# Two thirds of the cross-attention values by seven block products, W2 in single units, norm pieces in fewer steps

## The chip, the cores and the metric

The kernel runs on one core of a Trainium2 chip. A core has five engines that run at the same time and wait for each other through semaphores: TensorE (PE in the profile) multiplies matrices and writes to PSUM banks, VectorE (DVE) and ScalarE (ACT) do elementwise work, GpSimd (POOL) does a little of that and issues some transfers, SyncE (SP) issues most transfers. "PEld" are TensorE's weight loads, which run beside its matmuls. The metric is the device time of one execution in microseconds (us): 1362.22 us, the median of three runs from 1362.15 to 1363.08. All arithmetic is in fp32.

## The reference

A decoder layer on x of 16 batches of 112 tokens with 512 features. Three parts are added to x in turn, each applied to the normalized x:

```python
x = x + attn(layernorm(x))                      # 16 heads of 32, low-rank factors
x = x + xattn(layernorm(x), ctx_2048, mask)     # ctx: 16 x 375 x 512
x = x + ffn(layernorm(x))                       # 512 -> 2048 -> 512

# xattn
q, k, v = hs @ Wq.T + bq, at @ Wk.T + bk, at @ Wv.T + bv     # at = ctx
scores = clip(where(attend, clip(q . k / sqrt(32)), -10000), -50, 50)
probs  = softmax(scores);  probs = probs / (probs.sum() + 1e-8)
delta  = rs * ((probs . v) @ Wo.T + bo)
delta  = (delta - mean) / sqrt(var + eps) * ln_gamma + ln_beta
# ffn
out = fwht(silu(x @ W1.T) * (x @ W3.T)) @ W2.T               # fwht over 2048
```

The Hadamard transform (fwht) of the hidden layer is applied to W2 instead, once for all tokens. Each of the 16 batches has 375 context tokens whose keys and values (512 features each) have to be computed: this is the work that the change touches.

## The kernel before

The profiled function is `decoder_layer` with its body `finite_layer`; a second path for input that isn't finite exists and doesn't run. There are three stages: self-attention to about 304 us, cross-attention to about 823 us, the feed-forward part to the end.

TensorE's instructions stand in an order written out by hand (`tc.manual_schedule`). The other engines' order is made by a scheduler, which places each instruction by when it expects its operands; on each engine instructions then start strictly in that order. `tc.issue_after(x)` keeps instructions behind x in it. A class `Filler` holds a queue of generators, each a series of small pieces of TensorE work; `fill(us)` runs pieces of it worth so many microseconds, `drain` all that are left. `mixed(a, b, n)` takes pieces of two generators in turn after n pieces of the first.

**The cross loop.** Iteration b attends batch b and, as filling, makes keys and values of batch b+1. The 375 tokens are three chunks of 125 (KP). A step (b, kc) of `Cross.step` has the scores of chunk kc (matmuls L925), their exp on ScalarE (L1326) with a scale and a bias per token that carry the mask (tiles `scl`, `bia`, laid out by token and chunk), the weighing of the values of the chunk before (L936), and the sum of the exponentials on VectorE (L1356). At kc = 0 the batch before is divided: `key_sums` (L947) sums the exponentials over tokens into one PSUM bank, four reciprocals (L1368) read it, and one operation (L1369) multiplies. Behind each step the filling runs.

**Values and keys.** `token_rows` (L898) makes the values of a chunk: 4 matmuls of 512 columns with the chunk's context as weights, then a copy on VectorE (L903). `Seven.biased` (L1005) makes the keys of a batch (512 features, 376 columns, the last one a zero) by seven products of blocks of 256 features and 188 tokens, in place of eight, as Strassen's method does. For this it needs sums of blocks of the weight (tile `xks`, once) and of the context (tile `kt`, L975, four operations of 2 x 188 columns per batch). A product is 4 matmuls of 188 columns. VectorE gathers the products into `kT` (L1058 to L1092), some with the keys' bias bk or with the difference of its halves, dbk. Two of the three held banks accumulate several products. The context of batch b+2 is loaded by one transfer at the start of iteration b (L1214), and GpSimd clears the last column.

**Other work in the loop.** Queries of two batches at odd b (L880). At b = 0, 4, 8 the output projection of a group of four batches (L909) and afterwards its norm and residual (`finish` pieces: at bl = b mod 4 > 0, two per step). W2 has two phases. Up to b = 8 its four halves (`W2Half`) are loaded, multiplied with a small Hadamard matrix (L1627, scaled by L1628) and combined by butterflies (L1643, L1644), one pair per step. From b = 9 on, `W2Piece` reads four quarters of two units each (2 x 256 columns) from what the halves stored (L1660, tile `w2i`), makes six sums of them (L1671 to L1686, tiles `w2i` and `w2o`) and stores each (L1669), two operations per step: four pieces. At b = 14 and 15 the first blocks of the feed-forward part are loaded, and their sums (L965) made.

**Buffers.** PSUM tag "mm" has 3 banks, which nearly all filling and the key sums take in turn. Weights, `xks`, `kt`, W2's tiles and the first feed-forward blocks share 8 slots of 8 KB a partition (`weight`); context and keys share 4 (`big`); values have 5; rows of 512, among them the mask and the first normalized tiles, take slots of a ring (`row`).

## Time and profile before

| | |
|---|---|
| three runs | 1362.15, 1362.22, 1363.08 us |
| profiled execution | 1362.72 us |
| span of its profile | 1360.9 us |
| granted TensorE clock | 0.998 of full speed |
| busy: PE, DVE, ACT, POOL | 1340.7, 820.6, 440.6, 38.0 us |
| L898 on the context (values, cross) | 178.8 us in 384 records |
| L1005 (keys, cross) | 106.8 us in 600 records |
| context loads | 16 of 750 KB, 4.8 us to landing |
| W2 piece loads, stores | 16 of 256 KB, 24 of 256 KB |

A row of the page's groups reads: line, engine, operation, output <- input by tile names, shapes (for a matmul the weights' rows x columns, then the output), number of records; busy us, mean ns of one; idle time of the engine just before them, and what ended it. Each fp32 matmul leaves two records. Rows of the waits read: who waited, for what, the total in us, how often, the longest. Rows of the timeline read: start in us, length in us, engine, line, operation, and how many records are drawn together. "SPq" is SyncE's queue, which holds the issue of transfers.

### The profile page before, as it was taken

Reading aid. Unit: us, or ns where it says so; the run is one execution under the profiler, and the core shown is the slowest. Engines: PE = TensorE matmul, PEld = TensorE weight load, DVE = VectorE, ACT = ScalarE, POOL = GpSimd, SP = SyncE. Lnnn points to the kernel's source line nnn. Section 1 sums busy time; section 2 is a strip of 40 time slices with the busy share of each in tenths; the row PEclk is TensorE's granted clock in tenths of the full one; section 3 lists DMA queues with packets and bytes.
Section 4 is the critical chain, followed back from the end, with each engine's and each line's share of the span. In section 5 each row is a group of like instructions: output and inputs, shape, how many; then the busy total and the mean of one; then the engine's idle time right before and its main releaser. Section 6 shows DMA issues by size and latency. Waiting matters only on the chain.

```text
span 1360.9 us, 20404 instructions
## 1 busy us (share of the span) xinstructions
PE 1340.7 (99%) x8472; PEld 834.1 (61%) x8472; DVE 820.6 (60%) x1571; ACT 440.6 (32%) x859; POOL 38.0 (3%) x68
## 2 busy tenths in 40 slices
PE   8999999999999999999999999999999999999997
PEld 5587776665767577756777765545555555555553
DVE  4487768735565686669675668557653245554332
ACT  3355453643444334433545452201110011111000
POOL 2000100310000100000000000000000000000000
PEclk9999999999999999999999999999999999999999
DMA  7000022110103011103342111111031122322201
GB/s 249 1 1 1 22 80 71 31 47 24 55 24 124 16 55 62 55 1 109 108 136 97 39 48 32 47 46 47 32 124 62 47 62 70 92 77 79 92 0 57
DMA packets 63898, 82.44 MB, mean 61 GB/s; under 512 B 3105, under 2 KB 48177, under 8 KB 61365
## 3 DMA queue, kind: packets, MB, share of 16 engines
q1 hardware_dynamic: 62128, 77.83, 17.4%
q0 software_dynamic: 672, 1.62, 0.4%
q8 instruction: 69, 1.13, 0.3%
q10 hardware_dynamic: 996, 1.59, 0.3%
q14 instruction: 33, 0.26, 0.1%
HBM read 65.83 MB, written 15.20 MB: 60 GB/s over the span
## 4 chain that ended last, share of the span: by engine, by line
PE 94%; DVE 4%; ACT 1%; DMA 1%; issue 1%; DVEq 0%; ACTq 0%; POOLq 0%
PE mm L898 15%; PE mm L1005 14%; PE gate L1538 12%; PE mm L909 7%; PE ys L1538 7%; PE gate L1472 6%; PE mm L880 6%; PE mm L1538 5%; PE sc L925 5%; PE ys L936 4%; PE ys L1472 4%; PE mm L1472 3%; PE sc L1192 2%; PE mm L841 1%; PE mm L1627 1%; PE mm L947 1%
## 5 line engine op out<-in xcount | busy, mean ns | idle before, releaser
L898 PE MATMUL mm<-xv,cT 128*125 128x512 f32 x384 | 178.8, 602 | 0.8 <-DVE v L903 0.8
L1326 ACT ACTIVATE e<-sc,bia,scl 125x896 f32<-125x896 f32 x64 | 68.4, 1094 | 171.3 <-PE sc L925 171.3
L898 PEld LDWEIGHTS mm<-xv,cT 128*125 128x125 f32 x384 | 68.4, 187 | 76.4 <-issue 71.8
L1330 ACT ACTIVATE sc<-sc,limit,nscl 125x896 f32<-125x896 f32 x96 | 102.6, 1068 | 0.0
L1538 PE MATMUL gate<-t,f 128*128 128x448 f32 x256 | 101.5, 539 | 0.0
L1356 DVE TENSOR_TENSOR es<-es,e 125x896 f32<-125x896 f32 x64 | 68.4, 1090 | 49.1 <-ACT e L1326 49.1
L1472 PE MATMUL gate<-h,f 128*128 128x448 f32 x224 | 86.6, 540 | 0.0
L1538 PE MATMUL gate<-xyT,f 128*128 128x448 f32 x192 | 80.1, 540 | 0.0
L1538 PEld LDWEIGHTS gate<-t,f 128*128 128x128 f32 x256 | 48.8, 190 | 47.4 <-issue 46.9
L1162 ACT ACTIVATE e<-sc,mx 112x112 f32<-112x112 f32 x256 | 64.3, 402 | 41.7 <-DVE mx L1158 41.7
L1538 PE MATMUL ys<-t,f 128*128 128x448 f32 x192 | 77.4, 539 | 0.0
L1005 PEld LDWEIGHTS mm<-kt,xks 128*128 128x128 f32 x360 | 59.1, 190 | 15.3 <-issue 14.8
L1472 PEld LDWEIGHTS gate<-h,f 128*128 128x128 f32 x224 | 42.6, 190 | 41.2 <-issue 40.8
L1554 ACT COPY u<-gate 128x448 f32<-128x448 f32 x16 | 8.5, 531 | 182.3 <-PE gate L1538 109.4
L1005 PE MATMUL mm<-kt,xks 128*128 128x188 f32 x360 | 63.5, 324 | 0.0
L1538 PEld LDWEIGHTS ys<-t,f 128*128 128x128 f32 x192 | 36.6, 190 | 35.6 <-issue 35.4
L1484 DVE TENSOR_TENSOR h<-h,h 128x896 f32<-128x896 f32 x32 | 32.8, 1086 | 40.9 <-PE ys L1472 31.6
L1538 PEld LDWEIGHTS gate<-xyT,f 128*128 128x128 f32 x192 | 36.1, 190 | 34.3 <-issue 33.7
L898 PE MATMUL mm<-wv,xyT 128*112 128x512 f32 x128 | 56.9, 595 | 0.0
L925 PEld LDWEIGHTS sc<-q,kT 32*125 32x125 f32 x1536 | 46.2, 183 | 15.5 <-issue 13.2
L925 PE MATMUL sc<-q,kT 32*125 32x112 f32 x1536 | 54.7, 279 | 0.0
L1538 PE MATMUL mm<-xyT,f 128*128 128x448 f32 x128 | 53.4, 540 | 0.0
(237 smaller groups left out, 2211.2 us busy)
## 6 DMA issues: line engine op xcount, KB each, us to landing
f<-in_f_w SPq DMA_DIRECT2D x64, 256.0 KB, 3.2
f<-blocks SPq DMA_DIRECT2D x14, 1024.0 KB, 4.8
cT<-in_ctx SPq DMA_DIRECT2D x16, 750.0 KB, 4.8
w<-in_f_w SPq DMA_DIRECT2D x4, 1024.0 KB, 6.1
w<-w SPq DMA_DIRECT2D x4, 1024.0 KB, 4.6
w2i<-w SPq DMA_DIRECT2D x16, 256.0 KB, 4.1
blocks<-w2o SPq DMA_DIRECT2D x12, 256.0 KB, 2.4
blocks<-w2i SPq DMA_DIRECT2D x12, 256.0 KB, 2.4
```

Source lines behind the costliest of these rows:

```text
L880: nc.tensor.matmul(acc[:, :n], w[:, c, ts(j, P)], src[:, c, :], start=(c == 0), stop=(c == C - 1))
L898: nc.tensor.matmul(acc[:n, :], src[:, c, :], w[:, c, :], start=(c == 0), stop=(c == C - 1))
L909: nc.tensor.matmul(acc, xyT[:, c, ts(t, P)], w[:, c, :], start=(c == 0), stop=(c == C - 1))
L925: nc.tensor.matmul(views[i // 2][:, i % 2, j, :], k_of(i, j), q_of(i, j), start=True, stop=True)
L936: nc.tensor.matmul(y[ts(i, DH), j, :], v[:, HG * j + i, :], es[i // 2][:n, i % 2, j, :], start=first and j == 0, stop=last, skip_group_che ...
L1005: nc.tensor.matmul(acc[:, m], lhs[:, k, ts(m, P)], rhs[:, k], start=first and m == 0 and k == 0, stop=k == 1, skip_group_check=True,)
L1162: nc.scalar.activation(e[:, i, j, :], sc[:, i, j, :], AF.Exp, scale=SCALE, bias=mx[:, i, j : j + 1],)
L1326: nc.scalar.activation(es[i], sc, AF.Exp, scale=scl[:, n : n + 1], bias=bia[:, n : n + 1])
L1330: nc.scalar.activation(sc, sc, AF.Relu, scale=nscl[:, n : n + 1], bias=limit[:KP, :1], accum_out=low[:KP, 2 * n + i : 2 * n + i + 1],)
L1356: self.last = nc.vector.tensor_tensor(total, total, late[3][i][:KP], ALU.add).ins
L1472: nc.tensor.matmul(banks[m][bank], o[:, c, ts(m, P)], t[:, c, :], start=first and c == 0, stop=c == UNITS - 1, skip_group_check=True,)
L1538: nc.tensor.matmul(bank, o[:, s, k, :], t[:, k, :], start=first and k == 0, stop=k == 1, skip_group_check=True,)
```

## The change

Values. For batches 1 to 15 the values of the first two thirds are no longer 2 chunks x 4 matmuls of 512 columns: `Seven.rows` makes them by seven products of 125 x 256, with the context blocks (or the keys' `kt` sums of them) as weights and blocks of xv, or sums of those in a new tile `xvs`, as moving operand. The first product of a column is copied, the others added by VectorE, with the block order changed so that the same `kt` sums serve keys and values. To this end the columns of the context are laid out anew: [chunk 0 | 63 columns of chunk 2 | chunk 1 | the other 62 of chunk 2 | the first 63 again]. Each half of 188 columns then begins with a whole chunk, and the last 125 columns are chunk 2. The load is five transfers in place of one. The third chunk of the keys has to be contiguous: GpSimd copies 63 columns (4 x 63 a partition) behind the keys (`whole`), and its clearing of the last column goes. The mask is laid out to match, by three transfers into two row tiles. The values of the third chunk, and all of batch 0's, stay `token_rows`. `pieces` gives the order: third chunk first, then a product of values and one of keys in turn.

Keys. Each product of `Seven` has a bank of its own and none accumulates over products; two bias copies become one, and one more add takes its place.

W2. A half is loaded after b = 0, 2, 4, 6 (before: ahead of the loop, and after b = 1, 3, 5), a step runs two pairs of butterflies (before: one), from b = 9 four operations (before: two). `W2Piece` is one unit (256 columns): eight pieces, each in one slot `w2p`, its results in place.

Others. Norm pieces run in the steps kc = 1 and 2 only. The sums of the first feed-forward blocks are made at the end of b = 14.

In the changed kernel L898 becomes L908, L1005 L1012, L947 L957, L1368 L1422, L975 L985, L1628 L1684, L1643 L1699, L1671 L1725, L1660 L1716; the new products of values are L1105, their copies L1108, adds L1110, GpSimd's copy L1253.

```diff
-    mi = row("mi").bitcast(I32)[:KP, : B * KC]
-    nc.gpsimd.dma_start(out=mi, in_=mask_t)
+
     scl, nscl, bia = (keep.tile([KP, B * KC], F32, name=n) for n in ("scl", "nscl", "bia"))
-    nc.gpsimd.tensor_scalar(scl, mi, 0.5, SCALE, op0=ALU.is_gt, op1=ALU.mult)
+    parted = (S2 + 1) // 2 - KP
+    for kcs, parts in (
+        (slice(0, KC), ((0, 0, KP),)),
+        (slice(KC - 1, KC), ((0, parted, KP - parted), (KP - parted, 0, parted))),
+    ):
+        mi = row("mi").bitcast(I32)[:KP, : B * KC]
+        for to, start, n in parts:
+            nc.gpsimd.dma_start(out=mi[ds(to, n)], in_=mask_t[ds(start, n)])
+        m, sc_, bi = (
+            t.rearrange("p (b k) -> p b k", k=KC)[:, :, kcs] for t in (mi, scl, bia)
+        )
+        nc.gpsimd.tensor_scalar(sc_, m, 0.5, SCALE, op0=ALU.is_gt, op1=ALU.mult)
+        nc.gpsimd.tensor_scalar(bi, m, 0.5, 50.0, op0=ALU.is_gt, op1=ALU.mult)
     nc.gpsimd.tensor_scalar(nscl, scl, -1.0, None, op0=ALU.mult)
-    nc.gpsimd.tensor_scalar(bia, mi, 0.5, 50.0, op0=ALU.is_gt, op1=ALU.mult)
     nc.gpsimd.tensor_scalar(bia, bia, -50.0, None, op0=ALU.add)
 
...
-            a = self.bank(n)
-            took = product(a, a11, b11, True)
-            copy(c21, a, 1)
+            took = n * 8 / 1150.0
+            acc = self.product(a11, b11)
+            for m in range(2):
+                nc.vector.tensor_scalar(
+                    c21[:, m], acc[:, m], bias[:, 2 + m : 3 + m], None, op0=ALU.add
+                )
             yield took
-            b = self.bank(n)
-            took = product(b, s[:, 1], t[:, 1], True)
-            for m in range(2):
-                nc.vector.scalar_tensor_tensor(
-                    c12[:, m],
-                    in0=b[:, m],
-                    scalar=over[:, m : m + 1],
-                    in1=c21[:, m],
-                    op0=ALU.add,
-                    op1=ALU.add,
-                )
+            add_over(c11, self.product(a12, b21), c21)
             yield took
-            took = product(a, a12, b21, False)
-            copy(c11, a, 0)
+            add(c12, self.product(s[:, 1], t[:, 1]), c21)
             yield took
-            took = product(b, s[:, 2], t[:, 2], False)
-            add(c22, b, c21, ALU.add)
+            add(c22, self.product(s[:, 2], t[:, 2]), c12)
             yield took
-            d = self.bank(n)
-            took = product(d, s[:, 0], t[:, 0], True)
-            add(c22, d, c22, ALU.add)
+            add(c21, self.product(a22, t[:, 3]), c22)
             yield took
-            took = product(b, a22, t[:, 3], False)
-            add(c21, b, c21, ALU.add)
+            acc = self.product(s[:, 0], t[:, 0])
+            add(c22, acc, c22)
+            add(c12, acc, c12)
             yield took
-            took = product(d, s[:, 3], b22, False)
-            add(c12, d, c12, ALU.add)
+            add_over(c12, self.product(s[:, 3], b22), c12)
             yield took
+        def rows(self, dst, src, t):
+            n = dst[0].shape[0]
+            c11, c12, c21, c22 = (dst[k][:, ts(d, 2 * P)] for d in range(2) for k in range(2))
+            b11, b12, b21, b22 = src
+            (a11, a12, a21, a22), s = self.blocks, self.s
+            for w, x, *sums in (
+                (a11, b11, (c21, None)),
+                (a12, b21, (c11, c21)),
+                (s[:, 1], t[:, 1], (c12, c21)),
+                (s[:, 2], t[:, 2], (c22, c12)),
+                (a22, t[:, 3], (c21, c22)),
+                (s[:, 0], t[:, 0], (c22, c22), (c12, c12)),
+                (s[:, 3], b22, (c12, c12)),
+            ):
+                acc = psum("mm", [P, D])[:n, : 2 * P]
+                for k in range(2):
+                    nc.tensor.matmul(acc, x[:, k, :n], w[:, k], start=k == 0, stop=k == 1)
+                for c, more in sums:
+                    if more is None:
+                        nc.vector.tensor_copy(c, acc)
+                    else:
+                        nc.vector.tensor_tensor(c, acc, more, ALU.add)
+                yield 0.9
...
         def __init__(self, b):
             self.b, self.v = b, []
             self.c = big("cT")
-            nc.sync.dma_start(out=self.c[:, :, :S2], in_=ctx_t[b])
-            nc.gpsimd.memset(self.c[:, :, S2 : 2 * HK], 0.0)
+            self.x = self.c[:, :, : 2 * HK]
+            parted = HK - KP
+            for to, start, n in (
+                (0, 0, KP),
+                (KP, 2 * KP, parted),
+                (HK, KP, KP),
+                (HK + KP, 2 * KP + parted, KP - parted),
+                (S2, 2 * KP, parted),
+            ):
+                nc.sync.dma_start(
+                    out=self.c[:, :, ds(to, n)], in_=ctx_t[b][:, :, ds(start, n)]
+                )
+        @staticmethod
+        def third(ap, kc):
+            return ap[..., ds(min(kc, 1) * HK + max(kc - 1, 0) * KP, KP)]
+        def whole(self):
+            nc.gpsimd.tensor_copy(self.k[:, :, S2 : HK + 2 * KP], self.k[:, :, KP:HK])
         def sums(self):
-            self.x = self.c[:, :, : 2 * HK]
             self.t = sums_tile("kt", HK)
             t_sums(self.t, *quarters(self.x))
         def first_keys(self):
             self.k = big("kT")
-            yield from features(self.k, xk, self.c[:, :, :S2], S2, bk)
-        def keys(self):
+            yield from features(self.k, xk, self.x, 2 * HK, bk)
+            self.whole()
+        def third_of_values(self, kc):
+            v = values("v")
+            self.v.append(v)
+            yield from token_rows(
+                v[:KP], xv, self.third(self.c, kc), nc.vector.tensor_copy
+            )
+        def values(self):
+            for kc in range(KC):
+                yield from self.third_of_values(kc)
+        def pieces(self):
             self.k = big("kT")
-            yield from xks.biased(self.k, self.x, self.t, bk, dbk)
-        def values(self, kcs=range(KC)):
-            for kc in kcs:
-                v = values("v")
-                self.v.append(v)
-                yield from token_rows(
-                    v[:KP], xv, self.c[:, :, ts(kc, KP)], nc.vector.tensor_copy
-                )
+            keys = xks.biased(self.k, self.x, self.t, bk, dbk)
+            self.v = [values("v") for _ in range(2)]
+            rows = xvs.rows(
+                [v[:KP].rearrange("p h r -> p (h r)") for v in self.v],
+                quarters(self.x),
+                self.t,
+            )
+            last = self.third_of_values(KC - 1)
+            for _ in range(2):
+                yield next(last)
+            for _ in range(7):
+                yield next(rows)
+                yield next(keys)
+            self.whole()
...
             scs = scores(
-                lambda i, j: keys.k[ds(i * DH, DH), j, ts(kc, KP)],
+                lambda i, j: keys.third(keys.k[ds(i * DH, DH), j], kc),
...
-        behind = tc.issue_after(done[-2]) if len(done) > 1 else nullcontext()
-        with behind:
-            s_sums(o[:, 4:], *(o[:, k] for k in range(4)))
         return o
+    def block_sums(o):
+        s_sums(o[:, 4:], *(o[:, k] for k in range(4)))
...
-            self.c = ds(c, 2)
-            self.x = sums_tile("w2i", 2 * P)
+            self.c = c
+            self.x = block_tile("w2p").rearrange("p s k m -> p s (k m)")
             for k in range(4):
-                nc.sync.dma_start(out=self.x[:, k], in_=halves[k][:, self.c])
+                nc.sync.dma_start(out=self.x[:, k], in_=halves[k][:, c])
         def steps(self):
-            x0, x1, y0, y1 = (self.x[:, k] for k in range(4))
-            o = sums_tile("w2o", 2 * P)
-            a, e, g = (o[:, k] for k in range(3))
+            x0, x1, y0, y1, a, e, g = (self.x[:, k] for k in range(7))
             tt, st = nc.vector.tensor_tensor, nc.vector.scalar_tensor_tensor
...
+    xvs = Seven("xvs", xv)
...
-    halves2 = [W2Half(0)]
+    halves2 = []
     def w2_steps():
...
             yield from halves2[k].steps()
         while b < 9:
             yield
-        for c in range(0, UNITS, 2):
+        for c in range(UNITS):
             yield from W2Piece(c).steps()
     w2_work = w2_steps()
...
                 finish = c.finish()
             us += 13.0 if g < 3 else 0.0
         if b + 1 < B:
-            f.add(mixed(kv[b + 1].values(), kv[b + 1].keys(), 2))
+            f.add(kv[b + 1].pieces())
             if b % 2:
                 queries = qs[(b + 1) // 2].pieces()
                 us += 6.0
...
             cross.step(b, kc, qs[b // 2].q, kv[b], f, us / KC)
             if (b, kc) > (0, 1):
                 with tc.issue_after(cross.last):
-                    for _ in range(2 if bl > 0 else 0):
+                    for _ in range(2 if bl > 0 and kc > 0 else 0):
                         next(finish, None)
-                    for _ in range(1 if b < 9 else 2):
+                    for _ in range(2 if b < 9 else 4):
                         next(w2_work, None)
         f.drain()
-        if b in (1, 3, 5):
-            halves2.append(W2Half(b // 2 + 1))
+        if b in (0, 2, 4, 6):
+            halves2.append(W2Half(b // 2))
+        if b == B - 2:
+            with tc.issue_after(cross.last):
+                for o in ready.values():
+                    block_sums(o)
     for _ in w2_work:
         pass
     cross.weigh(cross.late)
```

## The prediction

> **What bounds the kernel now.** I read the page's busy shares first, then the chain that ended last, then the groups by form, the waits, and last the timeline and windows of the cross stage (about 304 to 823 us), which holds nearly all of the change.
>
> ```profile
> PE 1340.7 (99%) x8472; PEld 834.1 (61%) x8472; DVE 820.6 (60%) x1571; ACT 440.6 (32%) x859; POOL 38.0 (3%) x68
> ...
> PE 94%; DVE 4%; ACT 1%; DMA 1%; issue 1%; DVEq 0%; ACTq 0%; POOLq 0%
> ```
>
> TensorE is busy 1340.7 of the span's 1360.9 us. So every microsecond of matmul taken out is a microsecond won, unless TensorE then waits. VectorE has 40% spare, but only as a mean.
>
> ```profile
> L898 PE MATMUL mm<-xv,cT 128*125 128x512 f32 x384 | 178.8, 602 | 0.8 <-DVE v L903 0.8
> L1005 PE MATMUL mm<-kt,xks 128*128 128x188 f32 x360 | 63.5, 324 | 0.0
> L965 DVE TENSOR_TENSOR f<-f 128x256 f32<-128x256 f32 x128 | 48.8, 419 | 2.0 <-DMA f<-in_f_w 1.2
> L1368 DVE RECIPROCAL r<-mm 128x112 f32<-128x112 f32 x64 | 47.8, 809 | 7.7 <-PE mm L947 7.7
> ```
>
> The first row is the work that shrinks: TensorE hardly waits for its copies (0.8 us in all). Each fp32 matmul leaves two records that overlap, so the mean of 602 ns is not its price. That comes from runs of equal records in the timeline:
>
> ```profile
> 658.71 5.41 PE L898 MATMUL mm<-xv,cT 128*125 128x512 f32 x12
> ...
> 649.84 6.22 PE L880 MATMUL mm<-xyT,xq 128*128 128x224 f32 x32
> ...
> 642.57 2.71 PE L1005 MATMUL mm<-kt,xks 128*128 128x188 f32 x16
> ```
>
> Less the overhang of the last record, starts lie 429 ns apart at 512 columns, 189 at 224 and 159 at 188: columns divided by 1.2 per ns, and about 2 ns. At 256 columns that makes 215 ns (estimate). In the window from 700 to 720 us TensorE is busy 20.00 of 20 us at clock 1.00. The starts later than this spacing show stalls of 4.1 us in the whole cross stage, 13.7 in the program.
>
> **What the change takes off TensorE.** Per batch 1 to 15, two thirds of the values are 8 matmuls of 512 columns, two records each: 8 x 2 x 0.429 = 6.87 us. In their place stand 7 products of 2 matmuls of 256: 14 x 2 x 0.215 = 6.03. The difference is 0.84 us, times 15 = **12.5 us gained**. The keys' products keep their number and width; that they no longer accumulate over two products changes nothing for TensorE. Batch 0, scores, the feed-forward stage: unchanged, 0.
>
> **What it puts on VectorE.** Per batch two copies of 512 leave (0.60 apart in runs) and one of 256 and seven adds of 256 come (0.34 each, between 0.33 of 188 and 0.46 of 376 columns, and below the 0.42 of the L965 row): +8 x 0.34 - 2 x 0.60 = +1.5. Keys: two bias copies fewer, two adds with bias more (same width, 0.33), one add of 376 more: +0.46. With one unit of W2 in place of two (48 operations of 256 for 24 of 512) and waits between dependent halves it comes to about +2.4 us per batch, some 36 us in all. TensorE has 25.4 us per batch afterwards, VectorE about 17 of work: as a mean it keeps up. So the question is one of order: where does VectorE come late?
>
> **How much lateness is free.** TensorE writes to three banks in turn. One holds the key sums (L947) until four reciprocals (L1368) have read it.
>
> ```profile
> 380.35 0.93 PE L947 MATMUL mm<-es,ones 125*32 125x448 f32 x8
> ...
> 378.21 1.28 DVE L1628 TENSOR_SCALAR w<-mm 128x512 f32<-128x512 f32 x2
> 379.41 0.68 DVE L1644 SCALAR_TENSOR_TENSOR w<-w 128x512 f32<-128x512 f32 x1
> 380.01 0.68 DVE L1643 TENSOR_TENSOR w<-w 128x512 f32<-128x512 f32 x1
> 380.73 0.69 DVE L1644 SCALAR_TENSOR_TENSOR w<-w 128x512 f32<-128x512 f32 x1
> 381.37 2.99 DVE L1368 RECIPROCAL r<-mm 128x112 f32<-128x112 f32 x4
> ```
>
> Here the sums end at 381.28 and the reciprocals start at 381.37. Before, three halves of values (3 x 1.72 = 5.15 us) passed until the bank was wanted, so the reciprocals could start 5.15 - 2.99 = 2.1 us late. After, it is 4 matmuls of 512 (3.43) and one block product (0.86): 4.29, so 1.2 us (a little is for the release). In the timeline of before this lag is above 1.2 us in 8 of 16 batches, up to 2.98. These would lose the excess, but most of it was norm pieces, which leave the reciprocals' step.
>
> **Where it comes late.** I laid the changed order of VectorE, with the spacings above, against TensorE's, place by place. Estimates, each a stall put back on TensorE:
>
> - *Start, 1.0 us (0.5 to 2.5).* Two mask tiles in place of one take slots of the ring that the first normalized tiles need; GpSimd's queue gets two more DMAs and two more small operations. The first matmul chain starts at 17.97 and has nothing before it to hide this.
> - *W2 halves, steps (2,0) and (6,0), 1.8 each, 3.6.* Two steps of W2 per key chunk place seven or so butterflies (L1643, L1644) instead of three ahead of the reciprocals: 4 x 0.68 = 2.7 us late, less 1.2, and 0.3 to restart. In (4,0) and (8,0) other projections cover it.
> - *Norm at batch 5, 1.5.* Its chain of small operations (0.2 each) and the end of its residual adds stand before the reciprocals: lag 2.7, less 1.2.
> - *W2 pieces from batch 9, 10.9.* All data of a piece now live in one slot, so the loads of the next wait for its six stores:
>
> ```profile
> DVE w2o L1671 <- DMA w2i<-w: 11.9, 3, 7.4
> ...
> 656.78 3.40 SPq L1660 DMA_DIRECT2D w2i<-w  x4
> ...
> 663.91 0.69 DVE L1671 TENSOR_TENSOR w2o<-w2i 128x512 f32<-128x512 f32 x1 [2.04 <-DMA w2i<-w]
> ...
> blocks<-w2o SPq DMA_DIRECT2D x12, 256.0 KB, 2.4
> ```
>
> From the first load's issue to the first use took 7.1 us at 256 KB; at half the bytes I take 5.0. A store takes 2.4. Between the last operation of one piece and the first of the next VectorE has in order four reciprocals (2.99), L1369 (0.55) and two copies (0.60 + 0.34): 4.5 us. So it stands still for 2.4 + 5.0 - 4.5 = 2.9 us, with the first key eviction behind it, for which TensorE soon waits since two banks give it about 2 us. Batch 9, with both pieces: 3.0. Batch 10, where moreover the keys' sums (kt) take a slot whose stores must land (2.5): 4.9. Batch 11: 0.65. Batch 12, where a wait stands directly before the reciprocals but VectorE reaches it early: 2.35. Before, pieces used two slots and twelve stores, and the like wait cost nothing or 0.6 (the gap at 631).
> - *Others, 2.4 (1 to 6).* The values of a batch now have nine evictions, not three, and each bank must come free within two products, also behind an es add of 1.02 us.
>
> Sum: 1.0 + 3.6 + 1.5 + 10.9 + 2.4 = **19.4 us lost**. The 4.1 us of old stalls are contained in it.
>
> **What I put at nothing.** The GpSimd copy of kT (15 times) is needed first by the third key chunk, a third of a batch later. But while GpSimd ran four operations of 512 (5.69 us, 1.42 each), VectorE's L1643 took 1.66 instead of 0.68. [...] By the row a hit costs 0.98 per 1.42 us of GpSimd, here 0.5, so 7 us. [...]
>
> The context load becomes five transfers per batch.
>
> ```profile
> cT<-in_ctx SPq DMA_DIRECT2D x16, 750.0 KB, 4.8
> ```
>
> 2560 packets of 250 to 500 bytes replace 512 of 1500. At the 27 ns that 512-byte packets took this is 2560 x 27 / 16 = 4.3 us of the engines, and 4 x 0.55 = 2.2 of issue in SP's queue: landing 2 to 3 us later. [...] W2Half(0)'s loads, moved from ahead of the loop to behind batch 0, and those after it stand in SP's queue behind a context load, 2 us more, with a batch of lead; the sums of the first feed-forward blocks (L965 row, 0.42 each) move to the end of batch 14 where W2 is done; the norm pieces, at two thirds of their rate, still end batches ahead of the feed-forward stage. All three 0; where the cover fails, one or two tenths of a microsecond per operation.
>
> **Sum.** -12.5 - 4.1 + 19.4 = +2.8 on the profiled execution's 1362.72. The median is 0.5 lower, 1362.22, so **1365.0 us**.
>
> **Rivals.** A difference of 0.2% (2.7 us) is about what a measurement can tell from none: faster is below 1359.5, slower above 1364.9.
>
> A, *VectorE keeps up* (faster): the scheduler's order does not bite, since waits fall where three banks carry TensorE. For it: VectorE is idle a third of each batch, and its 36 us more fit there. The stalls then shrink to 4 to 9 us: 1362.2 - 16.6 + (4 to 9) = 1350 to 1355; with half of my losses 1355. Against it: the built order puts waits directly ahead of reciprocals and evictions. It decides once the losses are under 13.9 us.
>
> B, *the pieces' round trip is worse* (slower): each of seven hand-overs costs the 2.9 us (20.3) and the kt sums wait 2.5 more in four batches (10): 30, two thirds of it uncovered, 20 in place of 10.9, so 1365 + 9 = 1374. It decides from a round trip of 7.4 us on, if VectorE brings no lead to it. For it: stores and loads share SP's in-order queue with context loads. Against: VectorE is often early there.
>
> C, *a wash*: losses of 14 to 19 us, 1359.5 to 1364.9.
>
> D, that the change doesn't do what it says: weights of 125 columns load in 187 ns (L898 weight loads), below 215, so TensorE isn't bound by loading; I give this 2%, at 1367 or more.
>
> **Chances.** Forecast (losses 19 to 24 us, 1365 to 1370) 0.33; B 0.17; D 0.02; C 0.17; A 0.31. Faster 0.31, same 0.17, slower 0.52. The range leaves out 0.1 at A's low end and 0.1 above B's middle: 1352 to 1375; the likeliest case alone has 1362 to 1370.
>
> **What the profile after would show.** L898's busy time falls to about three eighths and rows of 256-column products, 420 records together, appear; their starts are 215 ns apart (if 230, 6 us of the gain go). The stalls: the first query matmul near 19.0 instead of 17.97; gaps before the second or third product after the key sums in batches 2, 5 and 6; waits of VectorE on w2p's loads of 2 to 5 us in batches 9 to 12, with TensorE gaps just behind them. The prediction is wrong if those waits stand there and TensorE does not stop, or if gaps appear in plain batches 13 to 15, where I count none.

## The result, and the profile after

The changed kernel takes 1372.34 us (median of four runs, 1370.09 to 1374.92) against 1362.34 before: a ratio of 1.0073, 95% interval 1.0052 to 1.0094. It is 10 us slower; the forecast was 2.7 us slower, with 1352 to 1375 as its range. The profiled execution took 1370.99 us, its span 1369.2.

The page after, its busy shares and the chain that ended last:

```profile
span 1369.2 us, 21160 instructions
PE 1337.0 (98%) x8652; PEld 868.8 (63%) x8652; DVE 856.8 (63%) x1704; ACT 440.3 (32%) x859; POOL 50.6 (4%) x72
...
PE 88%; DVE 6%; ACT 2%; issue 2%; DMA 1%; POOL 1%; SPq 0%; DVEq 0%; ACTq 0%; POOLq 0%
```

TensorE's part of the chain went from 94% to 88%: it waits more. VectorE has the 36 us more of work that the prediction had (856.8 against 820.6). The groups by form that answer to those shown before:

```profile
L908 PE MATMUL mm<-xv,cT 128*125 128x512 f32 x144 | 66.3, 602 | 0.0
L1105 PE MATMUL mm<-xvs,kt 128*125 128x256 f32 x180 | 46.9, 383 | 1.3 <-DVE kT L1067 1.0 <-DVE kT L1055 0.2
L1110 DVE TENSOR_TENSOR v<-mm,v 125x256 f32<-125x256 f32 x105 | 42.8, 420 | 5.3 <-PE mm L1105 4.3
L1422 DVE RECIPROCAL r<-mm 128x112 f32<-128x112 f32 x64 | 47.8, 810 | 10.0 <-PE mm L957 10.0
```

The plain value matmuls fell to three eighths (384 records to 144), and the new products start 0.216 us apart in the timeline: the matmul part is as forecast. Measured from one batch's key sums (L957) to the next (a *segment* below), the batches without late work on VectorE are 0.6 to 1.0 us shorter than before, as 0.84 says. The 10 us come from a few places. The timeline shows three where TensorE stood still for over 2 us; in each VectorE was late with the reciprocals. Below, the *lag* of a batch is the time from the end of its key sums to the start of its reciprocals. Step (4,0), VectorE's rows and then TensorE's:

```profile
447.39 2.35 DVE L1699 TENSOR_TENSOR w<-w 128x512 f32<-128x512 f32 x2
449.67 1.28 DVE L1700 SCALAR_TENSOR_TENSOR w<-w 128x512 f32<-128x512 f32 x2
450.87 0.68 DVE L1699 TENSOR_TENSOR w<-w 128x512 f32<-128x512 f32 x1
451.58 0.69 DVE L1700 SCALAR_TENSOR_TENSOR w<-w 128x512 f32<-128x512 f32 x1
452.19 2.98 DVE L1422 RECIPROCAL r<-mm 128x112 f32<-128x112 f32 x4
455.09 0.63 DVE L1699 TENSOR_TENSOR w<-w 128x512 f32<-128x512 f32 x1
455.64 0.61 DVE L1423 SCALAR_TENSOR_TENSOR xyT<-ys,r 128x448 f32<-128x448 f32 x1
```

```profile
447.19 7.13 PE L919 MATMUL mm<-xo,xyT 128*128 128x512 f32 x16
456.40 5.37 PE L919 MATMUL mm<-xo,xyT 128*128 128x512 f32 x8 [2.07 <-DVE xyT L1423]
```

The key sums ended at 447.26; W2's butterflies hold the reciprocals up by 4.93 us, and the output projection, which needs xyT, waits. Step (12,0):

```profile
722.96 0.42 DVE L1740 TENSOR_TENSOR w2p<-w2p 128x256 f32<-128x256 f32 x1
730.01 0.43 DVE L1725 TENSOR_TENSOR w2p<-w2p 128x256 f32<-128x256 f32 x1 [6.63 <-DMA w2p<-w]
730.47 0.43 DVE L1728 TENSOR_TENSOR w2p<-w2p 128x256 f32<-128x256 f32 x1
730.81 2.99 DVE L1422 RECIPROCAL r<-mm 128x112 f32<-128x112 f32 x4
```

```profile
733.90 2.85 PE L1012 MATMUL mm<-cT,xk 128*128 128x188 f32 x8 [2.44 <-issue]
```

From the last operation of one W2 piece to the first of the next pass 7.05 us, of which VectorE waits 6.63 for the load. The sums were ready at 726.96, and TensorE stood until 733.90, 2.61 us by the starts. The third place is step (5,0), where the chain of small norm operations ran from 482 to 490.9 ahead of the reciprocals: 2.43 us.

What I had not counted follows behind these waits. The windows (columns: stretch; its length; busy us of PE, PEld, DVE, ACT, POOL; granted TensorE clock; DMA share; GB/s):

```profile
450.00:455.00 5.00, 4.32 (x11) 1.58 (x9) 4.96 (x8) 0.00 (x0) 0.00 (x0) 1.00 0.00 0
455.00:460.00 5.00, 3.60 (x5) 1.50 (x6) 5.00 (x11) 0.76 (x2) 0.00 (x0) 0.71 0.00 0
...
495.00:500.00 5.00, 5.00 (x20) 4.53 (x20) 2.17 (x7) 0.74 (x2) 0.00 (x0) 0.70 0.01 3
500.00:505.00 5.00, 5.00 (x82) 4.38 (x81) 1.95 (x4) 2.45 (x3) 0.00 (x0) 1.00 0.00 0
```

Behind each of the three waits matmuls take twice their time for 3.41 us (starts 0.85 us apart instead of 0.43 at 512 columns, 0.43 instead of 0.216 at 256): the granted clock is 0.71 and 0.70 over the five from 455 and from 495, which is 0.5 for 2.95 and 3.01 of them, and 0.50 from 733.53 to 736.94 behind the wait of step (12,0) (the last section has a whole stretch). By the spacings this costs 1.54, 1.61 and 1.29 us, 4.4 together. The mean clock of the execution is 0.995 against 0.998, and three thousandths of 1369 us are 4.1.

### The profile page after: what moved, and what is told of

It reads as the page before. It is cut to its first block, busy times and chain, and to the rows that moved or that the text cites. A ratio compares the mean times of both kernels' runs of the same rounds, so it can differ in the third digit from the quotient of the medians.

```text
span 1369.2 us, 21160 instructions
## 1 busy us (share of the span) xinstructions
PE 1337.0 (98%) x8652; PEld 868.8 (63%) x8652; DVE 856.8 (63%) x1704; ACT 440.3 (32%) x859; POOL 50.6 (4%) x72
## 4 chain that ended last, share of the span: by engine, by line
PE 88%; DVE 6%; ACT 2%; issue 2%; DMA 1%; POOL 1%; SPq 0%; DVEq 0%; ACTq 0%; POOLq 0%
PE mm L1012 13%; PE gate L1594 12%; PE mm L908 7%; PE ys L1594 7%; PE mm L919 7%; PE gate L1526 6%; PE mm L1105 6%; PE mm L890 5%; PE mm L1594 5%; PE sc L935 4%; PE ys L1526 4%; PE ys L946 3%; PE mm L1526 3%; PE sc L1210 2%; PE mm L851 1%
## 5 line engine op out<-in xcount | busy, mean ns | idle before, releaser
L908 PE MATMUL mm<-xv,cT 128*125 128x512 f32 x144 | 66.3, 602 | 0.0
L1012 PE MATMUL mm<-kt,xks 128*128 128x188 f32 x360 | 65.1, 324 | 0.0
L1012 PEld LDWEIGHTS mm<-kt,xks 128*128 128x128 f32 x360 | 59.7, 190 | 2.9 <-issue 0.7
L908 PE MATMUL mm<-wv,xyT 128*112 128x512 f32 x128 | 56.9, 595 | 0.0
L919 PE MATMUL mm<-xo,xyT 128*128 128x512 f32 x112 | 52.3, 615 | 2.1 <-DVE xyT L1423 2.1
L1422 DVE RECIPROCAL r<-mm 128x112 f32<-128x112 f32 x64 | 47.8, 810 | 10.0 <-PE mm L957 10.0
```

Of the source, the lines that this page charges most:

```text
L908: nc.tensor.matmul(acc[:n, :], src[:, c, :], w[:, c, :], start=(c == 0), stop=(c == C - 1))
L919: nc.tensor.matmul(acc, xyT[:, c, ts(t, P)], w[:, c, :], start=(c == 0), stop=(c == C - 1))
L1012: nc.tensor.matmul(acc[:, m], w[:, k, ts(m, P)], x[:, k], start=k == 0, stop=k == 1)
```

## The experiments

My theory after this comparison, P: the block products gain what TensorE saves, and the loss is a matter of placement, side work (norm, W2) in front of the reciprocals. The rival, R: VectorE's extra work and W2's round trip through memory cost their time wherever they stand.

**e1, order behind the division.** In the code `issue_after(cross.last)` is meant to keep side work behind the step's last es add. But in step kc = 1 there is no es add, so the mark is still that of kc = 0, which lies ahead of the reciprocals. So the norm pieces do not leave the reciprocals, as the prediction took them to: those of kc = 1, and the W2 steps of kc = 0 and 1, could all be put ahead of them.

```diff
-                nc.vector.scalar_tensor_tensor(
+                self.last = nc.vector.scalar_tensor_tensor(
                     xyT[:, :, ts(b, S)],
...
-                )
+                ).ins
```

> The changed kernel with one edit: the mark behind which norm pieces and W2 operations are ordered becomes the multiplication that follows the four reciprocals, where a batch is divided. TensorE's order stays the same. Theory P (placement): the stalls come from side work that VectorE has in order between the last es add and the reciprocals, 2.5 to 4.9 us of lag in seven batches; the mark was not renewed at kc = 1, so pieces of two steps gather ahead of the reciprocals. Then the lags fall under 1.2 us, the stalls of 1.2 to 2.6 us in batches 2, 4, 5, 6 and 12 go with the half-clock stretches behind three of them, and the time is 1349 to 1355. Theory R (round trip, load): the waits for W2's stores and loads and the 36 us more of VectorE work cost what they cost, and the stalls turn up a step later: 1366 to 1374.

Measured: 1364.46 us (12 runs; 1.0016 of before, 1.0007 to 1.0025), 7.9 less than the changed kernel. Between the two bands, so both theories are half right. All lags but one fell to 0.1 us, and up to the key sums of batch 9 the kernel is 3.7 us ahead of the kernel before. Then W2's pieces cost it 5.02 and 4.18 us in two segments. VectorE's timeline shows how, and TensorE's behind it:

```profile
674.86 1.08 DVE L1410 TENSOR_TENSOR es<-es,e 125x896 f32<-125x896 f32 x1
678.53 1.01 DVE L985 TENSOR_TENSOR kt<-cT 128x376 f32<-128x376 f32 x2 [2.60 <-DMA blocks<-w2p]
679.46 0.54 DVE L1051 TENSOR_TENSOR kT<-mm,kT 128x376 f32<-128x376 f32 x1
```

```profile
676.24 1.44 PE L1012 MATMUL mm<-kt,xks 128*128 128x188 f32 x8
680.06 2.07 PE L1105 MATMUL mm<-xvs,cT 128*125 128x256 f32 x4 [2.38 <-DVE kT L1051]
```

The kt sums take the slot whose stores must land, VectorE waits 2.60 us, the key eviction behind it is late, and TensorE stops for want of a bank. This is the place in which the prediction had put 4.9 us for batch 10.

**e3, pieces in two steps of three.**

```diff
-                    for _ in range(2 if b < 9 else 4):
+                    for _ in range(2 if b < 9 else 6 if kc > 0 else 0):
```

> The changed kernel with the W2 operations from batch 9 on as six per step in the steps kc = 1 and 2 only, not four in each of the three. The order on VectorE differs mainly at one place: the first operation of a piece no longer waits for its load (6.63 us) directly ahead of the reciprocals of batch 11, in step (12,0). Theory P: that stall (2.61 us, and about 1.4 us at half clock) goes and nothing else changes: 1367 to 1369.5. Theory R: the same round trip is waited for elsewhere: 1371 to 1374.

Measured: 1367.91 us (6 runs), 4.4 less than the changed kernel. The segment of step (12,0), 3.27 us longer than before in the changed kernel, is 0.24 longer here. The time is in theory P's band, and this one wait and the half clock behind it are gone, 3.0 us by the segment. But "nothing else changes" did not hold: in step (10,0), where TensorE had stood 0.86 us, it now stands 2.52. The waits of 1.20 and 0.47 us a batch earlier are gone, so TensorE comes to this step sooner, but VectorE does not: the six operations of a piece, with 0.58 us for its load, stand ahead of the reciprocals, and their lag is 3.76 us instead of 2.10. As theory R has it, a part of the cost moved.

**e5, values by plain matmuls again.**

```diff
-            for _ in range(7):
-                yield next(rows)
-                yield next(keys)
+            yield from mixed(self.values(), keys, 2)
```

> The changed kernel with all three thirds of the values by plain matmuls again, taken in turn with the keys as before the change; context layout, W2, norm steps and mask as changed (the sums xvs are made but not used). It prices the block products alone. If they gain the 12.5 us of TensorE and their VectorE work costs nothing: 1383 to 1386. If the seven adds per batch are what makes VectorE late (about 1.5 us per batch): 1372 or below. I expect 1381 to 1385, as the late places are those of W2 and the norm.

Measured: 1369.41 us (5 runs; 1.0047 of before). I had expected 1381 or more: a miss, and the most instructive run. Taking the block products out does not make the changed kernel slower by 12.5 us; the median is even 2.9 us lower. Whether it is really faster stays open: the runs overlap (1367.41 to 1372.00 here, 1370.09 to 1374.92 there), and of the half clock, which is not the same in every execution (mean granted clock 0.996 to 0.999 here, 0.994 to 0.996 there), this profile has one stretch where the changed kernel's has three. Against the kernel before, all the rest of the change, with plain values, costs 6.8 us. The lags are no smaller (2.46, 2.83, 5.10, 2.95, 2.46 us for batches 1 to 5), but the same lag stops TensorE less. Batch 1 has nearly the same lag in both, 2.47 us in the changed kernel and 2.46 here. There TensorE stands 1.22 us in the changed kernel and 0.36 here:

```profile
385.51 2.98 DVE L1411 RECIPROCAL r<-mm 128x112 f32<-128x112 f32 x4
```

```profile
388.60 1.51 PE L1012 MATMUL mm<-cT,xk 128*128 128x188 f32 x8 [0.20 <-issue]
```

So the room is 2.10 us with plain values and 1.24 with block products: the 2.1 and 1.2 of the prediction. Other batches agree. Here lags of 2.83, 2.65 and 4.38 us gave waits of 0.73, 0.52 and 2.28; in the changed kernel lags of 3.68, 2.10 and 3.85 gave 2.43, 0.86 and 2.61. At such a place the products' gain, 0.84 us a batch, was paid back with the same 0.9 us, and three times the half clock came on top.

**e6, the kernel before with e1's edit**, the same two lines.

> The kernel before with the same edit of the mark as e1. It says how much of what e1 wins belongs to the change's own placement. The kernel before has lags of up to 3 us but only 4.1 us of stalls in the cross stage, of which 0.6 to 1 us each stand behind reciprocals: theory P gives 1359 to 1362, theory R no change, 1362.

Measured: 1363.64 us (12 runs; 1.0008, 0.9999 to 1.0016). No gain, and above both bands: with 2.1 us of room the order was no trouble before, and the work shifted behind the division stops TensorE there (1.66 and 1.47 us, which were not there before).

**e14, one piece per batch.** e1 with pieces in step kc = 1 only.

```diff
-                    for _ in range(2 if b < 9 else 4):
+                    for _ in range(2 if b < 9 else 6 if kc == 1 else 0):
```

> e1 (work ordered behind the division) with one further edit: from batch 9 on a whole W2 piece, six operations, in the step kc = 1 of each batch and none in the others. In e1 three stalls are left in batches 9 to 12 (1.69, 2.55 and 2.32 us, the second behind key sums that waited 2.60 us for the stores of a piece), where the round trip store, load or store, kt sums lies inside the same batch. Theory: with a batch between pieces stores and loads land under other work, these stalls and the half-clock stretch go, about 9 us, and the block products' gain shows: 1353 to 1357, below the kernel before (1362.6). Rival: VectorE has too much work in these batches in any order, and they stall again: 1361 to 1365.

Measured: 1365.71 us (8 runs, 1363.38 to 1370.68). A miss. The kt sums follow the piece at once in VectorE's order and wait for its stores in two batches (2.68 and 2.82 us), and the pieces left over for batches 14 and 15 make two more segments 2.9 and 5.0 us longer: in the first key evictions stand behind waits of 2.00 and 0.80 us for the loads of a piece, in the second the token sums of the feed-forward stage stand ahead of an es add. The round trip was a trouble in each of the four orders tried inside the cross stage, as theory R has it. The run is also the best view of the clock: its eight executions are of the same program, and their times follow the mean granted clock.

| mean granted clock | times, us |
|---|---|
| 0.999 | 1363.38, 1364.46, 1365.01, 1365.05 |
| 0.998 | 1366.37 |
| 0.996 | 1367.47, 1369.31 |
| 0.994 | 1370.68 |

**e12, e13 and e15, without W2.** The work on W2 left out of the changed kernel, of the kernel before, and of e1.

```diff
             for c in range(0, UNITS, 2):
-                flat = self.w[:, ds(c, 2)].rearrange("p c n -> p (c n)")
...
-            yield from W2Piece(c).steps()
```

> The changed kernel without the work on W2: its four halves are loaded and stored, but the products with the Hadamard matrix, the butterflies and all pieces are left out (the result is then not the layer's). With e13 it prices block products, norm steps and mask without W2: if what W2 adds to VectorE and its round trip make the loss, e12 is 6 to 12 us faster than e13, 1334 to 1341. If the block products themselves gain nothing, both agree within 2 us.

> The kernel before with the same work on W2 left out. Its 16 products with the Hadamard matrix (32 records of 0.43 us, 13.7 us) are gone, and few stalls: 1345 to 1349.

> e12 (the changed kernel with the work on W2 left out, so the result is not the layer's) with the mark of e1. e12 was only 2.4 us faster than e13; its trace shows stalls of 2.24, 2.25, 1.91 and 0.76 us where norm pieces stand ahead of the reciprocals. If the block products' 12.5 us are there and only late reciprocals hide them: 1337 to 1341, 7 to 11 us below e13 (1348.4). If the value adds themselves make VectorE late at other places: 1344 or more.

Measured: e12 1345.94, e13 1348.37, e15 1345.17 us (4 runs each). e13 is as expected; e12 and e15 are misses. Without W2 the change wins 2.4 and 3.2 us; the first is hardly clear of the runs' spread (1344.95 to 1348.44 for e12, 1348.16 to 1348.96 for e13). From the key sums of batch 0 on, e15's profile is 6.9 us ahead of e13's. The rest was lost up to there: in batch 0 the kt sums waited 3.22 us for the context load in its five parts, with a value add behind them for which TensorE stood 2.48 us. Two stores of a W2 half go out 3.6 us ahead of that load in this run, so the five parts may not be the only cause. That wait doesn't exist in the changed kernel, but it shows that the load which I put at nothing is hidden only where the order of the kt sums lets it. Stalls of 1.92 and 1.40 us (late reciprocals behind kt sums, a late key eviction) are most of the remainder.

**e7, longer divisions.** e14 with more reciprocals.

```diff
                     nc.vector.reciprocal(r[:, c], sums[:, c])
+                for _ in range({1: 3, 2: 4, 4: 5, 5: 6, 6: 3, 7: 4, 8: 5, 13: 7}.get(b, 0)):
+                    nc.vector.reciprocal(r[:, 0], sums[:, 0])
```

> e14 with repeated reciprocals of the first quarter (0.745 us each) behind the four of chosen batches: 3 in batches 1 and 6, 4 in 2 and 7, 5 in 4 and 8, 6 in 5, 7 in 13. They only delay when VectorE frees the banks, by 2.2 to 5.2 us; with 1.2 us of room TensorE should stand 1.1, 1.9, 2.6, 3.4 and 4.1 us. Theory T1: a wait costs its own length: 18 to 20 us more than e14. Theory T2: waits of 2.2 us and more can be followed by some 3.4 us at half clock, 1.7 us each; waits of 1.1 are not: 22 to 27 us more, and the windows behind the long ones show a granted clock near 0.7.

Measured: 1384.06 us (2 runs), 18.4 more than e14. The dose was not what I meant: VectorE's order put evictions between the repeated reciprocals, so the waits were shorter than planned (none to 3.3 us) and the two theories can't be told apart by the total. Its waits serve in the section on the clock below.

**e16, pieces in the feed-forward stage.** e1, with the pieces behind the blocks of the first feed-forward pass.

```diff
-                    for _ in range(2 if b < 9 else 4):
+                    for _ in range(2 if b < 9 else 0):
                         next(w2_work, None)
...
-    for _ in w2_work:
-        pass
...
             p.products(u, i)
+            with tc.issue_after(p.last):
+                for _ in range(4):
+                    next(w2_work, None)
...
     run(late)
+    run(w2_work)
```

> e1 with W2's eight pieces moved out of the cross stage into the first pass of the feed-forward stage, four operations behind each block of it, where slots are many, VectorE is busy 40% and W2 is first read some 100 us later. e1's stalls of batches 9 to 12 (segments 5.0 and 4.2 us longer than before the change) should go and nothing come in the feed-forward stage: 1351 to 1356, faster than the kernel before (1362.6). Rival: the pieces stop TensorE in the feed-forward stage as they did in the cross stage: 1360 to 1366.

Measured: **1354.50 us** (4 runs, 1353.88 to 1354.68), 0.9938 of before, 0.9922 to 0.9955: faster than both kernels. Its page:

```profile
span 1352.7 us, 21165 instructions
...
PE 94%; DVE 2%; ACT 2%; issue 1%; POOL 0%; DMA 0%; ACTq 0%; DVEq 0%; POOLq 0%
```

TensorE's part of the chain is 94% again, no wait of the cross stage is longer than 1.40 us, no half-clock stretch is left in the cross stage, and the runs lie within 0.8 us.

**e17, the kernel before with its pieces at the same place**, by the edit of e16 (with one step per key chunk below batch 9, as before).

> The kernel before with its four W2 pieces moved to the same place as in e16, four operations behind each block. Before, the pieces cost TensorE under 3 us in the cross stage: 1360 to 1362.5. It tells how much of e16 a kernel without block products would have too.

Measured: 1403.39 us (4 runs), a miss by 40. A piece of two units takes two of the eight slots, and the blocks of the feed-forward stage, which need the same slots, come late:

```profile
866.28 2.61 PE L1538 MATMUL mm<-xyT,f 128*128 128x448 f32 x3 [11.90 <-DMA f<-in_f_w]
```

So the single unit in one slot, which I had booked as a loss, is what makes e16's place possible; that is argued from the slots, not tried apart.

**e19, e16 with plain values**, the edit of e5 on top of e16.

> e16 with the values of all thirds by plain matmuls, that is e5's edit in a kernel whose VectorE is not late. In the changed kernel that edit made it 2.9 us faster (1372.3 to 1369.4), as if the block products cost more than they gain. Theory: they gain their 12.5 us of TensorE less the few stalls left in e16, and only lateness hid it: 1362 to 1366 here, 8 to 11 us slower than e16. Rival: their adds cost VectorE's time in any order: 1352 to 1358.

Measured: 1364.64 us (22 runs), 10.1 more than e16. With e5 this makes a square of four kernels:

| | side work as changed | side work moved (e1's mark, pieces in the feed-forward stage) |
|---|---|---|
| plain values | 1369.41 | 1364.64 |
| block products | 1372.34 | 1354.50 |

The same products win nothing in the left column and 10.1 us in the right one. But not all of the 10.1 is theirs. In the profiles e16 is 10.9 us ahead at the last key sums. Of this 1.5 stand at the end of self-attention, since e19's execution ran its first query matmuls at half clock, and 2.77 are one wait in batch 2, where VectorE waits for the context load in its five parts (as in e15 the stores of a W2 half went out shortly before it) and a key eviction behind it is late:

```profile
410.08 1.01 DVE L985 TENSOR_TENSOR kt<-cT 128x376 f32<-128x376 f32 x2 [4.38 <-DMA cT<-in_ctx]
```

That leaves 6.7 us for the products, less the waits that e16 itself still has. The gain of TensorE is real; it shows where VectorE is on time.

## Why the prediction was right, and where its sum was off

The direction and the mechanism were right: a gain of 12.5 us on TensorE, more than undone by VectorE's lateness at a few places. The size was off: losses of some 25 us (16.6 + 8.5 by the profiled executions' last matmul) where I had 19.4. The likeliest case, 1362 to 1370, missed the time; only the wide range, whose upper end was set by rival B, takes it in. And two errors offset each other by luck: the waits at W2's pieces came out 4.1 us smaller than forecast, and the half clock, 4.4 us, was not in the sum. With the pieces at their full forecast the time would have been some 1376 us (estimate: 1372.3 + 4.1), above the range. By the terms of the sum:

- *Gain 12.5.* The spacing of the products and the batches without late work (0.6 to 1.0 us each for 0.84) show it. As time, 6.7 us of the difference between e19 and e16 are its net, with the stalls left in e16 on the other side: 5.3 us, of which 0.85, 0.75 and 1.40 stand ahead of block products.
- *Start 1.0.* 2.0 by the end of self-attention, and for two reasons: 0.43 at the first query matmul (18.40 for 17.97), and the rest at 244 to 248 us, where TensorE waits 0.49, 0.56 and 0.59 for the softmax, which it did not before. The four sums xvs (0.69 each) run on VectorE just ahead, and the softmax's next reduction starts at 243.07 instead of 240.83. I had not counted the xvs sums. (At the key sums of batch 0 the kernel is only 1.01 behind, since the first block products stand before them.)
- *Room 1.2 us for late reciprocals.* 1.24 measured, and 2.10 with plain values.
- *W2 halves, 1.8 in (2,0) and (6,0).* 1.22 each. But "in (4,0) and (8,0) other projections cover it" failed: in (4,0) the projection itself needs the division's result, and it waited 2.24 us, behind 4.93 of lag. GpSimd's four operations of 512 ran at the same time (442.75 to 448.60), and a VectorE operation took 1.79 us instead of 0.69. In (8,0), lag 2.47, nothing stopped.
- *Norm at batch 5, 1.5.* 2.43: the lag was 3.68 and not 2.7.
- *W2 pieces, 10.9.* 6.8 of waits: in batch 9 1.20 and 0.47 (forecast 3.0), in batch 10 0.86, 0.39, 0.57 and 0.70 (4.9), in batch 11 none (0.65), in batch 12 2.61 (2.35). The places were right and the sizes too large; the wait of the kt sums for a piece's stores, put at 2.5 us, was 1.70 here and 2.60 in e1.
- *Others, 2.4.* About as forecast: twice 0.43 behind value adds, twice 0.71 where a transposition waits for ScalarE's copy of the queries, twice 0.28 behind a value copy, 2.8 in all. 1.0 of the 2.4 was an allowance of mine for GpSimd's copy of kT; no run shows it, and these waits stood in its place.
- *Half clock, not in the sum: 4.4 us.* This is the term that was missing. With the 2.24 of (4,0) and the 1.0 more at the start it outweighs what the pieces fell short. The terms listed here come to 23.1 of the 25 us; the rest are shorter waits that I did not list one by one.
- *GpSimd's copy of kT.* It did run beside kt sums in most batches, as feared: in seven of them such a sum took 0.62 us instead of 0.54, in two 0.74. A hit cost mostly 0.08 us (0.20 twice), where I had 0.5 by the row; so about 1 us of VectorE in all. The copy itself took 0.39 to 1.51 us. The row of the four longer GpSimd operations was repeated (1.79 for 0.69).
- *Context load, 0.* It held in the changed kernel, but e15 and e19 have waits of 3.22 and 4.38 us of VectorE for it (the kernel before has one, of 3.99 at 571 to 575). Its packets took 27 ns at 500 bytes and 18 at 248 to 252 (medians in the trace of the changed kernel); those of 512 bytes took 27.

Of the signs, the first query matmul came earlier than 19.0, the gaps in batches 2, 5 and 6 and behind W2's pieces came (with one wait for a load of 6.63 us, more than the 5 given), and none came in batches 13 to 15.

Rival B (1374, the pieces' round trip) came near the time by another way: its reason, the waits for W2's pieces, came to 6.8 us where it had 20. Rival A decides where its text said, at losses under 13.9 us: e16, whose losses are 1354.5 - (1362.3 - 16.6) = 8.8 us, is that kernel.

## What to carry to other kernels

Work added to an engine with spare time (here VectorE, busy 63%) is free only where nobody waits for that engine soon: before making TensorE faster, look how late the evicting engine may be, and how much of that room the shorter matmuls take away (here from 2.10 us to 1.24). An ordering mark has to be renewed in every step in which work is placed behind it. A round trip through memory belongs in a stage with spare slots and a late reader, not beside the tightest stage (here 1364.46 us in e1 and 1354.50 in e16), and a stall should be priced with the clock that may follow it (here 1.29 to 1.61 us behind stalls of 2.24 to 2.61).

## What the runs showed of the hardware

Behind some waits of TensorE, the shortest of them between 1.5 and 2.2 us, the traces show a granted clock of 0.50; I had counted such waits at their own length alone. Of the waits of TensorE of 0.9 us and more in the cross stages of the fourteen profiles:

| length of the wait | waits | with matmuls at half clock behind it | cost of that |
|---|---|---|---|
| 0.9 to 1.5 us | 23 | 0 | none |
| 1.5 to 2.2 us | 7 | 2 | 1.67 and 1.78 us |
| 2.2 to 3.3 us | 18 | 13 | 0.46 to 1.62 us |

The length alone does not tell them apart: 2.24 us in step (4,0) of the changed kernel was followed by half clock, 2.40 at the same place in e5 was not. The granted clock as the traces record it does. In each profile it changes only at whole multiples of 3.413 us from the start of its record (in the changed kernel the full-clock stretches are 132, 10, 69 and 184 of these *beats*), and each half-clock stretch of a cross stage is one beat long. The two waits by beats, first the changed kernel, then e5:

```profile
453.64:457.05 3.41, 1.34 (x4) 0.45 (x3) 3.41 (x7) 0.76 (x2) 0.00 (x0) 1.00 0.00 0
457.05:460.46 3.41, 3.41 (x6) 1.36 (x5) 3.41 (x7) 0.00 (x0) 0.00 (x0) 0.50 0.00 0
```

```profile
455.90:459.31 3.41, 1.45 (x4) 0.76 (x5) 3.34 (x8) 0.76 (x2) 0.00 (x0) 1.00 0.02 5
459.31:462.72 3.41, 3.41 (x10) 1.43 (x8) 1.82 (x4) 0.00 (x0) 0.00 (x0) 1.00 0.00 0
```

In the changed kernel the whole wait fell into one beat; in e5 it began 0.44 us before a beat ended, so the next one had less of it. With each matmul counted at the spacing of the prediction (columns divided by 1.2 per ns, and 2 ns), TensorE stood 2.31 us in the first of these beats and 2.04 in the other. In the changed kernel's cross stage the three beats ahead of half clock have 2.31, 2.50 and 2.24 us of this, and no other has more than 1.51. Over the 5491 full-clock beats of all fourteen profiles, the 21 in which it stood 2.15 us or more were all followed by half clock; of the 4 from 2.10 to 2.15 one was, of the others none. So in these profiles what looked like chance goes with where a wait falls among the beats. I read this off the traces afterwards; no run was made to test it.

The spread of a kernel's runs went with it: 1370.09 to 1374.92 us for the changed kernel at mean clocks of 0.996 to 0.994, and 1353.88 to 1354.68 at 0.998 and 0.999 for e16, whose profile has no wait above 1.40 us in the cross stage.
